# Local attention: dividing the softmax weights on ScalarE ahead of their transposes, instead of turning the divisors and dividing the outputs

## The chip, the cores and the metric

One core of a Trainium2 chip runs the whole kernel in one launch. The metric is the device time of that launch in microseconds (us), as the median of three runs. The engines are named as the profile names them: PE (TensorE, with PEld for its weight loads), DVE (VectorE), ACT (ScalarE), POOL (GpSimd) and SP (the queue that issues DMAs). All data is float32.

## The reference, cut to what matters

The model applies four blocks to x of shape (8, 512, 256), each with its own residual: an attention over all positions (a), a block of two layers of local attention and gated feedforward, a second attention (b), and the local block again. The change touches the local attention only. There, for each of 8 heads of width 64, with windows of 128 positions:

```python
q = l2norm(q) * qs;  k = l2norm(k) * ksc          # then rotary positions
bq = q.reshape(b, h, w, WINDOW, d) * QK_SCALE     # WINDOW = 128, w = 4
bk, bv = look_around(bk), look_around(bv)         # own window and the one before
sim = jnp.einsum('bhwid,bhwjd->bhwij', bq, bk)
sim = jnp.where(mask, -finfo.max, sim)
attn = jax.nn.softmax(sim, axis=-1)
out = jnp.einsum('bhwij,bhwjd->bhwid', attn, bv)
x = x + out.reshape(b, n, INNER) @ wo
```

A query of the first window sees one block of 128 keys, every other query two. The softmax's division can be done on the weights `attn` before the product with v, or on `out` after it.

## The kernel before, in words

The eight batches are worked in two groups of four. A group goes through stages: attention a, local attention and feedforward (twice), attention b, local attention and feedforward (twice). Local attention (`attention_f`) therefore runs eight times: the profile calls them f0x, f0y, f1x and f1y, each name holding two layers.

A stage has 16 tiles of 128 rows (four batches with four windows), and one step for each, with one more step to drain. A step (`a_step`) works on several tiles at once: the attention of tile `step`, the turning of queries and keys of tile `step + 1`, the products of queries, keys and values of tile `step + 2`, and the output projection of tile `step - 1`. `begin`, `rows` and `statistics` prepare the batches that follow. The eight heads of a tile are two units ("even" and "odd" unit), each a `quad` of four heads.

Each unit goes through these functions: `scores` (PE, L586) into PSUM; `maxima` (DVE, L608: adds the mask `near`, takes the maxima; then L618, a product of 128x4 numbers that gives `nm`); `exponentials` (ACT, at L229: four activations, with the sums of the rows as accumulators in `sums`); `turn` (PE, L652: the weights transposed into `ppt`); `keep_turned` (DVE, L663: copied to `pt`); `values` (PE, L677: the outputs, already transposed, into `o`).

For a tile as a whole, `divisors` takes the reciprocals of the sums (DVE, L690) and spreads them over a 128x512 tile `rb` (POOL, L692); `turn_divisors` transposes it (PE, L701, four transposes), `keep_divisors` copies it to `rt` (ACT, L707), and `normalize` multiplies the outputs with it (DVE, L713) to `oT`. `project` (PE, L721) and `add` (DVE, L728) end the tile.

Beside this stand `queries_and_keys` (PE, L489, tile `pqk`), `rotate` (DVE, L517 and L520, then two adds on POOL, L526), `squared` (ACT, L532), `norms` (DVE, L539, then POOL), `value` (PE at L489, tile `pv`, and an ACT copy, L548), `normalize_keys` (DVE, L553), `turn_tile` (PE, L562, tile `pqt`), `keep_tile` (ACT, L571 and L572: `qT` and `kT`) and `started` (two groups of transposes on PE, `pht`, each with an ACT copy, L482, to `hT`).

The order in which the functions stand in `a_step` is the order of each engine's queue: `order_keeper` ties each instruction of an engine to the one before it. Instructions of the next stage (`ahead`) come in at the steps that call it and at the end.

Scores, turned weights, `pqk` and `pqt` share three PSUM buffers (`ps_s`, tag "s"), the smaller products share one (`ps_mm`, tag "mm"), the outputs have one (`ps_o`).

Of the kernel before, what the change touches and what calls it, by code (L numbers as in the profile page):

```python
# [11 lines left out]
F32 = mybir.dt.float32  # L12
AF = mybir.ActivationFunctionType
# [4 lines left out]
P = 128  # L18
# [3 lines left out]
H, HD = 8, 64  # L22
# [22 lines left out]
def kernel(  # L45
# [27 lines left out]
    nc = tc.nc  # L73
# [16 lines left out]
    pool = ctx.enter_context(tc.tile_pool(name="work", bufs=2))  # L90
    ps_s = ctx.enter_context(tc.tile_pool(name="ps_s", bufs=3, space=PSUM))
    ps_mm = ctx.enter_context(tc.tile_pool(name="ps_mm", bufs=1, space=PSUM))
# [91 lines left out]
    ident = const.tile([P, P], F32, name="ident")  # L184
# [282 lines left out]
    def attention_f(batches, l, g, ys, first_layer):  # L467
# [4 lines left out]
        tiles = [(b, t) for b in batches for t in range(NT)]  # L472
        hTs, kTs, vs = {}, {}, {}
        qTs, rns, raws = {}, {}, {}
        ps, pts, sums, os, rts, ots = {}, {}, {}, {}, {}, {}

        def started(b):
            n = f"f{g}_{b}"
# [203 lines left out]
                            stop=(k == nb - 1),  # L682
                        )

        def divisors(at):

            b, w = tiles[at]
            n = f"f{g}_{b}_{w}"
            s = sums.pop(at)
            nc.vector.reciprocal(s, s)  # L690
            rb = pool.tile([P, H, HD], F32, tag="two", name=f"rb_{n}", bufs=5)
            nc.gpsimd.tensor_copy(rb, s.unsqueeze(2).to_broadcast([P, H, HD]))  # L692
            rts[at] = rb

        def turn_divisors(at):
            b, w = tiles[at]
            n = f"f{g}_{b}_{w}"
            rows = rts.pop(at).rearrange("p h d -> p (h d)")
            prt = ps_mm.tile([P, 4, P], F32, tag="mm", name=f"prt_{n}")
            for k in range(4):  # L700
                nc.tensor.transpose(prt[:, k, :], rows[:, k * P : (k + 1) * P], ident)  # L701
            rts[at] = prt

        def keep_divisors(at):
            b, w = tiles[at]
            rt = pool.tile([P, 4, P], F32, tag="two", name=f"rt_f{g}_{b}_{w}", bufs=5)
            nc.scalar.copy(rt, rts[at])  # L707
            rts[at] = rt

        def normalize(at):  # L710
            b, w = tiles[at]
            oT = pool.tile([P, 4, P], F32, tag="two", name=f"oT_f{g}_{b}_{w}", bufs=5)
            nc.vector.tensor_mul(oT, os.pop(at), rts.pop(at))  # L713
            ots[at] = oT

        def project(at):
# [13 lines left out]
        nt, nu = len(tiles), 2 * len(tiles)  # L730

        def on(f, at, count=nt):
            if 0 <= at < count:
                f(at)
# [17 lines left out]
        def a_step(step):  # L752

            even, odd = 2 * step, 2 * step + 1
            on(scores, even, nu)
            on(maxima, even, nu)
            on(queries_and_keys, step + 2)
            on(normalize_keys, step + 1)
            on(exponentials, even, nu)
            on(rotate, step + 2)  # L760
            on(values, even - 1, nu)
            on(turn_divisors, step - 1)
            on(keep_divisors, step - 1)
            on(squared, step + 2)
            on(scores, odd, nu)
            on(maxima, odd, nu)
            on(normalize, step - 1)
            on(turn, even, nu)
            on(keep_turned, even, nu)
            on(value, step + 2)  # L770
            on(norms, step + 2)
            on(turn_tile, step + 1)
            on(exponentials, odd, nu)
            on(keep_tile, step + 1)
            on(project, step - 1)
            on(values, even, nu)
            on(add, step - 1)
            on(divisors, step)
            on(turn, odd, nu)
            on(keep_turned, odd, nu)  # L780
            on(statistics, step + 5)
            on(rows, step + 4)
            on(begin, step + 3)

        def head():
            for step in range(-5, 0):
                a_step(step)
                yield

        def run(ahead):  # L790
            tables_of(EXP_TABLES)
            kept_order = order_keeper()
            for step in range(nt + 1):
                with kept_order():
                    a_step(step)
                    if step == 5 or nt - 6 < step < nt - 1:
                        ahead()
            for _ in range(6):
                ahead()
# [144 lines left out]
    def feedforward_block(batches, g, finish):  # L944

        ys = {}

        def attention(l):
            if l == 0:
                for b in batches:  # L950
                    ys[b] = resid.tile([P, NT, D], F32, tag=f"y{b % GROUP}", name=f"y_{g}_{b}")
            return attention_f(batches, l, f"{g}{l}", ys, l == 0)

        for l in range(DEPTH):
            yield lambda l=l: attention(l)
            yield lambda l=l: feedforward(batches, l, f"{g}{l}", ys, l == DEPTH - 1, finish)
# [500 lines left out]
```

## Time and profile before

| | |
|---|---|
| median of three runs | 4659.25 us (4655.93 to 4671.47) |
| profiled execution, its time and its span | 4656.03 us, 4654.2 us |
| granted TensorE clock over the span | 0.967 |
| PE busy | 4328.7 us, 93% |
| DVE busy | 3179.8 us, 68% |
| ACT busy | 2242.0 us, 48% |
| POOL busy | 1274.8 us, 27% |
| one batch of local attention, four steps (442.69 to 501.54) | 58.85 us |
| PE, DVE, ACT, POOL busy in it | 58.17, 47.07, 31.80, 26.40 us |

Busy times are sums of the instructions' durations on one engine. In the views of the trace a row has the start, the duration, the engine, the line, the operation and the tiles written and read; what stands in brackets is the idle time of that engine before the row, and the work whose end released it. Several instructions of one kind that follow each other are one row with a count. A view of stretches gives for each the busy time and the number of instructions of PE, PEld, DVE, ACT and POOL, then the granted clock.

### The profile page before, as it was taken

Reading aid. Unit: us, or ns where it says so; the run is one execution under the profiler, and the core shown is the slowest. Engines: PE = TensorE matmul, PEld = TensorE weight load, DVE = VectorE, ACT = ScalarE, POOL = GpSimd, SP = SyncE. Lnnn points to the kernel's source line nnn. Section 1 sums busy time; section 2 is a strip of 40 time slices with the busy share of each in tenths; the row PEclk is TensorE's granted clock in tenths of the full one; section 3 lists DMA queues with packets and bytes.
Section 4 is the critical chain, followed back from the end, with each engine's and each line's share of the span. In section 5 each row is a group of like instructions: output and inputs, shape, how many; then the busy total and the mean of one; then the engine's idle time right before and its main releaser. Section 6 shows DMA issues by size and latency. Waiting matters only on the chain.

```text
span 4654.2 us, 68773 instructions
## 1 busy us (share of the span) xinstructions
PE 4328.7 (93%) x26240; PEld 2644.2 (57%) x26240; DVE 3179.8 (68%) x7432; ACT 2242.0 (48%) x5228; POOL 1274.8 (27%) x1164
## 2 busy tenths in 40 slices
PE   9999999997778899999999999999977778999999
PEld 5666656654444466566566666566544444665665
DVE  5667737738988777377456686477389887773773
ACT  3345415516778655155133454254178775541551
POOL 0014314312222243134100242243122222431431
PEclk9999999998889799999999999999999887999999
DMA  2000000000000000000100000000000000000000
GB/s 78 1 21 3 23 22 4 21 6 19 1 1 1 18 4 4 5 22 12 50 29 1 19 3 23 21 3 23 3 20 1 1 1 19 3 5 17 8 3 23
DMA packets 51370, 63.51 MB, mean 14 GB/s; under 512 B 6369, under 2 KB 45793, under 8 KB 51041
## 3 DMA queue, kind: packets, MB, share of 16 engines
q1 hardware_dynamic: 51040, 59.11, 3.9%
q8 instruction: 208, 3.41, 0.3%
q14 instruction: 122, 0.99, 0.1%
HBM read 46.54 MB, written 4.19 MB: 11 GB/s over the span
## 4 chain that ended last, share of the span: by engine, by line
PE 74%; DVE 18%; ACT 5%; POOL 1%; issue 1%; DMA 0%; SPq 0%; POOLq 0%; ACTq 0%; DVEq 0%
DVE num_b L1137 4%; PE pu_g1x L854 3%; PE pu_g0x L854 3%; PE pu_g0y L854 3%; PE pu_g1y L854 3%; DVE r_b L1121 3%; PE s_a L381 3%; DVE pt_b L1172 3%; PE o_a L415 3%; PE ppt_a L398 3%; PE pqk_f0x L489 2%; PE pqk_f1y L489 2%; PE pqk_f0y L489 2%; PE pqk_f1x L489 2%; DVE t_b L1117 2%; PE pu_b L1000 2%
## 5 line engine op out<-in xcount | busy, mean ns | idle before, releaser
L1167 PE MATMUL ppt_b<-ident,num_b 128*128 128x128 f32 x1280 | 245.8, 314 | 195.2 <-DVE pt_b L1172 153.2
L1167 PEld LDWEIGHTS ppt_b<-ident,num_b 128*128 128x128 f32 x1280 | 152.3, 155 | 377.3 <-ACT num_b L229 124.5
L1129 POOL TENSOR_TENSOR num_b<-num_b,causal 128x256 f32<-128x256 f32 (+2 forms) x176 | 172.0, 977 | 699.6 <-ACT num_b L1127 530.7
L229 ACT ACTIVATE p_a<-s_a,nm_a 128x512 f32<-128x512 f32 x256 | 173.6, 683 | 303.0 <-DVE nm_a L385 303.0
L229 ACT ACTIVATE num_b<-num_b,most_b 128x512 f32<-128x512 f32 (+3 forms) x512 | 280.7, 553 | 42.6 <-DVE most_b L1147 40.4
L1137 DVE CUSTOM_DVE_ANT_0 num_b<-num_b,r_b 128x512 f32<-128x512 f32 (+3 forms) x512 | 257.2, 548 | 4.6 <-POOL num_b L1129 4.6
L1098 PE MATMUL den_b<-st_b,st_b 18*128 18x384 f32 (+3 forms) x1024 | 245.1, 531 | 7.6 <-DVE t_b L1117 5.1
L1172 DVE COPY pt_b<-ppt_b 128x512 f32<-128x512 f32 (+1 forms) x352 | 223.1, 634 | 25.1 <-PE ppt_b L1167 23.8
L229 ACT ACTIVATE r_b<-den_b 128x1024 f32<-128x1024 f32 (+1 forms) x176 | 166.2, 945 | 149.2 <-PE den_b L1098 93.8
L1098 PE MATMUL dot_b<-st_b,st_b 16*128 16x384 f32 (+3 forms) x1024 | 218.9, 533 | 1.6 <-ACT num_b L1127 1.1
L229 ACT ACTIVATE p_f1y<-p_f1y,nm_f1y,rn_f1y 128x256 f32<-128x256 f32 (+1 forms) x256 | 143.7, 564 | 136.1 <-DVE nm_f1y L618 124.5
L229 ACT ACTIVATE p_f0y<-p_f0y,nm_f0y,rn_f0y 128x256 f32<-128x256 f32 (+1 forms) x256 | 143.7, 563 | 133.9 <-DVE nm_f0y L618 122.2
L229 ACT ACTIVATE p_f1x<-p_f1x,nm_f1x,rn_f1x 128x256 f32<-128x256 f32 (+1 forms) x256 | 143.7, 564 | 129.8 <-DVE nm_f1x L618 112.6
L229 ACT ACTIVATE p_f0x<-p_f0x,nm_f0x,rn_f0x 128x256 f32<-128x256 f32 (+1 forms) x256 | 143.7, 563 | 129.1 <-DVE nm_f0x L618 117.5
L1117 DVE TENSOR_TENSOR t_b<-den_b,r_b 128x1024 f32<-128x1024 f32 (+1 forms) x176 | 196.6, 1117 | 11.5 <-ACT r_b L229 10.5
L1121 DVE SCALAR_TENSOR_TENSOR r_b<-t_b,r_b 128x1024 f32<-128x1024 f32 (+1 forms) x176 | 197.8, 1124 | 0.1
L385 DVE TENSOR_REDUCE nm_a<-s_a 128x2 f32<-128x1024 f32 x128 | 156.1, 1220 | 61.0 <-PE s_a L381 59.8
L229 ACT ACTIVATE r_b<-r_b 128x1024 f32<-128x1024 f32 (+1 forms) x176 | 172.4, 980 | 5.5
L398 PEld LDWEIGHTS ppt_a<-ident,p_a 128*128 128x128 f32 x1024 | 109.9, 141 | 98.1 <-ACT p_a L229 39.7
L1127 ACT ACTIVATE num_b<-dot_b 128x1024 f32<-128x1024 f32 (+1 forms) x176 | 164.6, 935 | 0.0
L400 DVE COPY pt_a<-ppt_a 128x1024 f32<-128x1024 f32 x128 | 155.4, 1214 | 2.6 <-PE ppt_a L398 2.5
L854 PE MATMUL pu_g0x<-hT_g0x,wg_0x 128*128 128x512 f32 (+1 forms) x352 | 156.6, 592 | 0.0
(361 smaller groups left out, 11025.1 us busy)
## 6 DMA issues: line engine op xcount, KB each, us to landing
x<-in_x SPq DMA_DIRECT2D x8, 512.0 KB
out<-x SPq DMA_DIRECT2D x8, 512.0 KB
wf_0x<-in_f_wqkv SPq DMA_DIRECT2D x2, 1536.0 KB
wf_0y<-in_f_wqkv SPq DMA_DIRECT2D x2, 1536.0 KB
wf_1x<-in_f_wqkv SPq DMA_DIRECT2D x2, 1536.0 KB
wf_1y<-in_f_wqkv SPq DMA_DIRECT2D x2, 1536.0 KB
wg_0x<-in_f_w SPq DMA_DIRECT2D x2, 1386.0 KB
wg_0y<-in_f_w SPq DMA_DIRECT2D x2, 1386.0 KB
```

Of the source, the lines that this page charges most:

```text
L229: i = nc.scalar.activation(out, in_, func, **more).ins
L398: nc.tensor.transpose(ppt[:, odd, k, :], p[:, odd, k * P : (k + 1) * P], ident)
L489: nc.tensor.matmul(dst.rearrange("p h d -> p (h d)"), lhsT=hTs[b][:, k, t * P : (t + 1) * P], rhs=wqkv[:, k, c * INNER : (c + 1) * INNER], ...
L854: nc.tensor.matmul(pu[: cols.stop - cols.start, c], lhsT=w1[:, k, cols], rhs=hT[:, k, :], start=(k == 0), stop=(k == 1),)
L1098: return nc.tensor.matmul(s[:, a, m * width : (m + 1) * width], lhsT=left[at, j, past:width], rhs=right[at, j, :width], start=True, stop=True,
L1117: nc.vector.tensor_mul(t[:, :, :cols], den[:, :, :cols], r[:, :, :cols])
L1121: nc.vector.scalar_tensor_tensor(r[:, :, :cols], t[:, :, :cols], 2.0, r[:, :, :cols], ALU.subtract, ALU.mult)
L1127: nc.scalar.activation(num[:, :, :cols], dot[:, :, :cols], AF.Square, scale=-0.5)
L1129: nc.gpsimd.tensor_add(own, own, causal.unsqueeze(1).unsqueeze(1).to_broadcast([P, 2, len(js), P]))
L1137: nc.vector.tensor_tensor_reduce(out=s4[:, a, m, :], in0=s4[:, a, m, :], in1=r4[:, a, m, :], scale=-1.0, scalar=LOWEST, op0=ALU.mult, op1= ...
L1167: nc.tensor.transpose(ppt[:, k, :], p[:, a, k * P : (k + 1) * P], ident)
L1172: nc.vector.tensor_copy(pt[:, a, :nblocks, :], ppt[:, :nblocks, :])
```

## The change

The divisors are no longer spread, turned and multiplied into the outputs. A new function `divided` takes the reciprocals of one unit's four sums on VectorE, and ScalarE multiplies the unit's weights with them in place, one activation (identity with a scale for each row) for each head, before the weights are turned. `keep_values` then only copies the outputs out of PSUM. The order of the step is written anew: the odd unit's weights are turned at the start of the next step, and the values' product and the other parts stand at other places.

```diff
-        def divisors(at):
-            ...
-        def turn_divisors(at):
-            ...
-        def keep_divisors(at):
-            ...
-        def normalize(at):
+        def divided(unit):
+
+            at, quad = divmod(unit, 2)
+            p, s = ps[unit], sums[at]
+            some = slice(4 * quad, 4 * quad + 4)
+            nc.vector.reciprocal(s[:, some], s[:, some])
+            for odd in range(2):
+                for j in range(2):
+                    h = 4 * quad + 2 * j + odd
+                    nc.scalar.activation(p[:, odd, j], p[:, odd, j], AF.Identity, scale=s[:, h : h + 1])
+
+        def keep_values(at):
             b, w = tiles[at]
             oT = pool.tile([P, 4, P], F32, tag="two", name=f"oT_f{g}_{b}_{w}", bufs=5)
-            nc.vector.tensor_mul(oT, os.pop(at), rts.pop(at))
+            nc.vector.tensor_copy(oT, os.pop(at))
             ots[at] = oT
...
             on(scores, even, nu)
             on(maxima, even, nu)
+            on(turn, even - 1, nu)
+            on(normalize_keys, step + 1)
+            on(keep_turned, even - 1, nu)
             on(queries_and_keys, step + 2)
-            on(normalize_keys, step + 1)
             on(exponentials, even, nu)
+            on(divided, even, nu)
             on(rotate, step + 2)
             on(values, even - 1, nu)
-            on(turn_divisors, step - 1)
-            on(keep_divisors, step - 1)
             on(squared, step + 2)
             on(scores, odd, nu)
             on(maxima, odd, nu)
-            on(normalize, step - 1)
+            on(value, step + 2)
+            on(exponentials, odd, nu)
+            on(keep_values, step - 1)
             on(turn, even, nu)
             on(keep_turned, even, nu)
-            on(value, step + 2)
             on(norms, step + 2)
             on(turn_tile, step + 1)
-            on(exponentials, odd, nu)
             on(keep_tile, step + 1)
             on(project, step - 1)
+            on(divided, odd, nu)
             on(values, even, nu)
             on(add, step - 1)
-            on(divisors, step)
-            on(turn, odd, nu)
-            on(keep_turned, odd, nu)
             on(statistics, step + 5)
             on(rows, step + 4)
             on(begin, step + 3)
```

## The prediction

> **What bounds the kernel now.** The page's busy line comes first, then stretches of one stage. A stage is one layer of local attention (8 run, f0x to f1y with two layers each); its steps take one tile of 128 rows each, and one batch is four steps, w = 0 to 3. Below, w0 to w3 are the steps whose scores belong to that tile; w0 has one block of 128 keys, the others two. The third stretch is one batch, the other two are its steps w1 and w3 as the trace cuts them.
>
> ```profile
> PE 4328.7 (93%) x26240; PEld 2644.2 (57%) x26240; DVE 3179.8 (68%) x7432; ACT 2242.0 (48%) x5228; POOL 1274.8 (27%) x1164
> ...
> 456.46:470.14 13.68, 13.68 (x78) 8.40 (x80) 12.71 (x33) 7.54 (x21) 5.81 (x4) 1.00 0.00 0
> 486.71:501.54 14.83, 14.83 (x98) 9.68 (x100) 11.47 (x29) 7.93 (x22) 6.27 (x6) 1.00 0.00 1
> 442.69:501.54 58.85, 58.17 (x370) 37.52 (x372) 47.07 (x125) 31.80 (x87) 26.40 (x24) 1.00 0.00 1
> ```
>
> TensorE is busy in the whole of such a step (14.83 of 14.83 us), VectorE 11.5, ScalarE 7.9, GpSimd 6.3. "Busy" alone would not prove a bound, so I read the order of time. In a w3 step:
>
> ```profile
> 488.65 1.14 PE L586 MATMUL s_f0x<-kT_f0x,qT_f0x 64*128 64x256 f32 x8
> 489.71 3.70 PE L489 MATMUL pqk_f0x<-wf_0x,hT_f0x 128*128 128x512 f32 x8
> 493.45 1.22 DVE L517 TENSOR_TENSOR ro_f0x<-pqk_f0x,tab 128x1024 f32<-128x1024 f32 x1 [1.30 <-PE pqk_f0x L489]
> 494.37 0.66 PE L701 MATMUL prt_f0x<-ident,rb_f0x 128*128 128x128 f32 x4
> 495.95 2.50 POOL L526 TENSOR_TENSOR ro_f0x<-ro_f0x,rs_f0x 128x512 f32<-128x512 f32 x2 [5.51 <-DVE rs_f0x L520]
> 497.64 0.84 DVE L618 SCALAR_TENSOR_TENSOR nm_f0x<-nm_f0x,rn_f0x 128x4 f32<-128x4 f32 x1
> 498.40 0.68 DVE L713 TENSOR_TENSOR oT_f0x<-o_f0x,rt_f0x 128x512 f32<-128x512 f32 x1
> 499.54 1.96 PE L721 MATMUL pp_f0x<-wf_0x,oT_f0x 128*128 128x256 f32 x8
> ```
>
> Each PE row begins where the one before it ends: S (scores) 1.06, QK 3.63, V (values) 1.03, the turned divisors 0.58, S 1.07, T (turned weights) 0.93, the value product PV 1.72, the turned tile PQT 0.87, PP (projection) 1.89, then V and T again; 14.83 in all. So TensorE sets this step. But see a second chain: rotation starts 3.74 after QK (493.45), GpSimd's two adds run 495.95 to 498.45, and the tiny `nm` product of 128x4 takes 0.84 us instead of 0.16 because it ends only with them; L713 waits behind it. In the w1 step this chain is already the tighter one:
>
> ```profile
> 462.33 1.23 DVE L517 TENSOR_TENSOR ro_f0x<-pqk_f0x,tab 128x1024 f32<-128x1024 f32 x1 [0.25 <-PE pqk_f0x L489]
> 466.16 1.20 DVE L618 SCALAR_TENSOR_TENSOR nm_f0x<-nm_f0x,rn_f0x 128x4 f32<-128x4 f32 x1
> 467.28 0.68 DVE L713 TENSOR_TENSOR oT_f0x<-o_f0x,rt_f0x 128x512 f32<-128x512 f32 x1
> 468.11 1.97 PE L721 MATMUL pp_f0x<-wf_0x,oT_f0x 128*128 128x256 f32 x8
> ```
>
> `nm` asks 0.08 us after GpSimd's first add has ended (466.08) and pays the whole second one, 1.20 us. From the rotation's start to the projection's are 5.78 us, of which no part is slack: PP starts 0.15 after its operand. From QK's start that is 3.74 + 5.78 = **9.52 us**; in the w3 step TensorE itself needs 9.83 (489.71 to 499.54). The cover is 0.31.
>
> **What the Trainium skill says.** "SBUF — State Buffer", section "SBUF: two separate sides": the port pair of VectorE and GpSimd is an exclusive lock for a whole instruction, and a VectorE op with two SBUF inputs waits behind a GpSimd op that reads SBUF. The trace agrees (0.84 and 1.20 against 0.16). "ScalarE: Activation LUTs", section "What ACT_TABLE_LOAD costs": an ACTIVATE takes 186 ns + 0.833 ns per element, each pointer operand adds 93 ns, and neighbours overlap by 93 ns. The trace agrees where it can: an exp of 256 elements with two pointers took 590 ns (186 + 213 + 186 = 585). The same page, "Table sets", says that identity is in every set, so no table load is added; no run yet shows it. "PSUM — Partial Sum Buffer", "PSUM bank collisions raise a hardware error", says that two engines must not read a bank together; here Square (L532) indeed starts only when the rotation has ended (495.96 after 495.87).
>
> **The parts.** (1) Removed from each of 128 steps: four transposes on PE (0.58), one PSUM copy on ACT (0.58), one GpSimd copy (0.61). (2) VectorE: one reciprocal (0.19) becomes two; the product L713 (0.68) becomes a PSUM copy of the same size (L663 at 128x512: 0.68). (3) ScalarE gains eight identities. By the price above 186 + 213 + 93 = 492 ns each, 0.40 apart; I take 0.40 (estimate from the page). Bounds: 0.31 if the pointer is free, 0.585 if it costs what an exp with its accumulator does. ScalarE then has 7.9 - 0.6 + 3.2 = 10.5 of 14.5 us: not a bound by sum. (4) Waits: the reciprocal of the even unit stands on VectorE ahead of the rotation and waits for the exps; the identities of the odd unit stand on ScalarE ahead of the next batch's hT copies, and the turn of the odd unit moves to the next step's start, which covers them there. No DMA and no SP instruction moves; GpSimd's queue only loses its copy.
>
> **The new step, walked from S (even) at 0.** Maxima start 1.25 (489.90 - 488.65), exps 3.02, ends of the accumulators 5.48 (494.12 before). The reciprocal follows at 5.51, rotation may start at 5.61. In w2 and w3: S 1.06, T of the last odd unit 1.02, so QK starts at 2.06 and the rotation is due at 2.06 + 3.74 = 5.80: the new wait is hidden by QK with 0.2 to spare. From QK to PP, TensorE now needs 9.83 - 0.58 = 9.25, but the rotation chain still needs 9.52. So PP starts at 11.58, then 1.89 + 1.03 give **14.50** against 14.83: -0.33, not -0.58. Does anything else bind? Odd exps start 0.12 after `nm`, at 5.80 + 5.03 + 0.12 = 10.95; qT at 13.29, kT done at 14.33; the next S needs it at 14.50: fits by 0.17. Identities run 14.21 to 15.9; the turn in the next step starts its four pairs at 15.56, 15.8, 16.1, 16.3: fits at 0.40 each.
>
> w1: the turn ahead of QK belongs to w0 and is short (0.59), so QK starts at 1.65 and the rotation would be due at 5.39; the reciprocal holds it to 5.61. PP at 5.61 + 5.78 = 11.39, where TensorE would have been ready at about 10.6; V ends at 14.31. Then come the two transposes of the next batch with a ScalarE copy between, through one PSUM buffer:
>
> ```profile
> 471.96 0.60 PE L283 MATMUL pht_f0x<-ident,y_0x 128*128 128x128 f32 x4
> 472.59 0.58 ACT L482 COPY hT_f0x<-pht_f0x 128x512 f32<-128x512 f32 x1 [1.41 <-PE pht_f0x L283]
> 473.23 0.65 PE L283 MATMUL pht_f0x<-ident,y_0x 128*128 128x128 f32 x4 [0.68 <-ACT hT_f0x L482]
> ```
>
> Before, ScalarE was free and this cost 473.82 - 471.96 = 1.86. Now the copy stands behind the odd identities: exps 10.76, qT 13.10, kT 13.56, identities 14.02 to 15.62; copy 15.62 to 16.20, second turn 16.26, next S 16.84. Before: 473.82 - 457.53 = 16.29. So **+0.55**.
>
> w0: loses the divisors (0.59) and its own odd turn (0.59), gains w3's (1.02); -0.16, and 0.2 more in a first layer, where PQT waited for Square, which the later rotation of w1 behind the rows' normalization (1.66 on VectorE) gives back. Its `nm` is ready earlier and gets in between GpSimd's two adds, as before (0.50), so no bubble.
>
> A batch: -0.16 + 0.55 - 0.33 - 0.33 = **-0.27**. A stage has three such, then w0 (-0.2) and w1 without the hT copies (-0.1). Its tail loses: without QK the steps are a pure chain, and the even identities (1.6) now stand between the even and the odd exps. Step 14 takes 12.8 by the same walk (odd maxima 6.95, odd exps 8.73, oT 9.2, PP 9.3, V 11.2, a turn for the next stage 12.2) against 544.08 - 532.68 = 11.4; the last step and the drain 18.05 against 17.6. Together +1.9. Bounds: 0 if the gated stage's products fill the gaps, +3 if none does. Stage: -0.8 - 0.3 + 1.9 = +0.8; eight stages **+6.4 us**. Everything else is untouched.
>
> The profiled execution took 4656.03 us (span 4654.2); the sum gives 4662.4. It lies 3.2 below the median of the runs (4659.25), so for a median I say **4666**. 0.3% is 14 us, about what a measurement of this kernel can tell from no change.
>
> **Rivals.** *The saving shows (faster).* It needs the rotation chain to loosen: if `nm` asks 0.1 us earlier it ends with GpSimd's first add, 1.25 earlier. Then w2 and w3 reach 14.25, w1 16.0 to 16.2: a batch is near -1.4 to -1.6, a stage 3 x -1.5 - 1.0 + 1.9 = -3.6, all -29 us: 4630; with the tail's cover too, -44: 4615. The bare floor, 128 x 0.58 = 74 us, isn't reached. For it: the margin is 0.08. Against: w1 shows the miss every time, and the order there is the new one. Chance 0.32.
>
> *The identities are dear (slower).* The place is ScalarE's queue at a step's end. Above 0.53 each, the turn at 1.06 of the next step waits: at 0.585 by 0.2 us a step, the hT copies by 4 x 0.185 = 0.74 a batch: a batch +1.3, a stage 3.9 + 0.6 + 2.5 = 7, all +56: 4715. Between 0.45 and 0.5 with the dear tail, +20 to +30: 4680 to 4690. For it: no identity with a pointer is in the trace, and each new wait is walked with little to spare (0.2, 0.17). Against: the page's price. Chance 0.40 of being over +14.
>
> *It doesn't do what it says:* identity missing from the set would add loads of 1.28 us each (the page's 20 loads took 25.7) hundreds of times; inside the slower case, under 0.02.
>
> **How the numbers follow.** The walk's own case, within 14 us, has 0.28: its centre is +6, but a term of 0.1 us a step is 13 us. The likeliest by its own bounds (identity 0.31 to 0.49, tail 0 to 3) spans 4641 to 4688. The range reaches into both rivals, 4620 to 4698, and leaves about 0.2 outside.
>
> **What would show it.** Right: PE busy falls by some 74 us but the span doesn't; `nm` of odd units at 1.2 us, PE idle ahead of L721 by 0.2 in w2 and w3 and by 0.8 in w1; the second transpose of hT waiting 1.3 us instead of 0.7; w2 and w3 at 14.50, batches near 58.4 (58.85 before). Wrong: w3 at 14.25, or `nm` at 0.5 and less (the first rival); identities 0.5 apart and PE waiting for them at the turn (the second).

## The result and the profile after

The changed kernel takes **4689.15 us** (median of 4 runs, 4683.71 to 4691.68) against 4657.85 for the kernel before beside it (4 runs, 4655.93 to 4671.47): a ratio of 1.0059, 95% interval 1.0038 to 1.0080. It is slower by 0.6%, twice what the measurement can tell from no change. Run once more on another occasion it took 4685.90, a ratio of 1.0041 (1.0029 to 1.0054). The forecast was 4666 in a range of 4620 to 4698, with 0.40 for slower, 0.32 for faster.

The profiled execution took 4683.71 us, its span is 4681.9 (before: 4656.03 and 4654.2), so **27.7 us** of span are to be explained; every split of it below is of these two executions. The granted TensorE clock is 0.960 (before 0.967). The page's busy line:

```profile
PE 4267.5 (91%) x25728; PEld 2608.4 (56%) x25728; DVE 3208.6 (69%) x7560; ACT 2575.3 (55%) x6124; POOL 1209.6 (26%) x1036
```

TensorE has 512 instructions less (4 x 128) and is busy for 61.2 us less, while the span grows. One batch of local attention, and its steps w1 and w2, in stretches that begin with a step's first scores (columns: length, busy time of PE, PEld, DVE, ACT, POOL with the number of instructions, clock, DMA share, GB/s):

```profile
441.74:499.67 57.93, 55.59 (x356) 35.79 (x354) 47.71 (x129) 42.20 (x116) 24.61 (x19) 1.00 0.00 1
454.98:471.70 16.72, 14.63 (x91) 9.23 (x89) 12.39 (x33) 12.23 (x33) 8.07 (x5) 1.00 0.00 0
471.70:486.09 14.39, 14.26 (x94) 9.28 (x93) 11.86 (x29) 9.99 (x26) 3.27 (x6) 1.00 0.01 2
```

The batch is 0.92 us *shorter* than before (58.85), although the kernel is slower. TensorE no longer fills its steps: 2.1 us of w1 are idle. The w2 step in order of time:

```profile
473.69 3.60 PE L489 MATMUL pqk_f0x<-wf_0x,hT_f0x 128*128 128x512 f32 x8
477.12 0.18 DVE L690 RECIPROCAL sums_f0x<-sums_f0x 128x4 f32<-128x4 f32 x1 [0.84 <-ACT p_f0x L229]
477.33 1.23 DVE L517 TENSOR_TENSOR ro_f0x<-pqk_f0x,tab 128x1024 f32<-128x1024 f32 x1
477.33 1.71 ACT L694 ACTIVATE p_f0x<-p_f0x,sums_f0x 128x256 f32<-128x256 f32 x4 [0.25 <-DVE sums_f0x L690]
479.89 2.51 POOL L526 TENSOR_TENSOR ro_f0x<-ro_f0x,rs_f0x 128x512 f32<-128x512 f32 x2 [8.07 <-DVE rs_f0x L520]
481.15 1.27 DVE L618 SCALAR_TENSOR_TENSOR nm_f0x<-nm_f0x,rn_f0x 128x4 f32<-128x4 f32 x1
482.34 0.68 DVE L699 COPY oT_f0x<-o_f0x 128x512 f32<-128x512 f32 x1
483.17 1.97 PE L707 MATMUL pp_f0x<-wf_0x,oT_f0x 128*128 128x256 f32 x8
```

From QK (L489) to the rotation 3.64 us, from the rotation to the projection 5.84: the chain of the prediction, with the `nm` product of 128x4 now at 1.27 us. The turned tile starts at 482.00 and takes 0.87 where nothing follows late (498.67 to 499.54 before), so TensorE is free at 482.87 and waits 0.30 for the projection's operand. (Rows of TensorE overlap a little; by their own ends the gap is 0.13.) Four identities take 1.71 us. In w1 the same chain is later still, and the hT copy waits behind the odd unit's identities:

```profile
464.28 1.27 DVE L618 SCALAR_TENSOR_TENSOR nm_f0x<-nm_f0x,rn_f0x 128x4 f32<-128x4 f32 x1
466.30 1.97 PE L707 MATMUL pp_f0x<-wf_0x,oT_f0x 128*128 128x256 f32 x8 [0.85 <-DVE oT_f0x L699]
468.88 1.71 ACT L694 ACTIVATE p_f0x<-p_f0x,sums_f0x 128x256 f32<-128x256 f32 x4
470.49 0.57 ACT L482 COPY hT_f0x<-pht_f0x 128x512 f32<-128x512 f32 x1
471.11 0.66 PE L283 MATMUL pht_f0x<-ident,y_0x 128*128 128x128 f32 x4 [1.24 <-ACT hT_f0x L482]
```

So the full steps behave as walked, and gain. The loss lies in the stages' ends and in the clock. Step 13 is the last w1 of a stage, step 14 the w2 after it. Steps from scores to scores in one second-layer stage (f0y), before and after: w1 16.29 and 16.72, w2 and w3 14.83 and 14.39, w0 12.68 and 12.44; but step 13 takes 16.14 and 16.76, step 14 11.40 and **12.69**, and from the last step's scores to the feedforward's first output (the row y, DVE L900, after L885) 42.32 and **44.24**. From the last feedforward's row of this kind to its own, that stage is 259.61 and 260.85 long, and it is the only one of the four second-layer stages that is so short after: the others take 262.4 to 262.9. What they have more is seen by setting the same place of two stages side by side. First stretches of 3.41 us, then TensorE's rows, of f0x (near 900) and f0y (near 2200):

```profile
896.57:899.98 3.41, 0.93 (x17) 0.85 (x16) 2.54 (x8) 2.45 (x8) 0.00 (x0) 1.00 0.00 0
899.98:903.39 3.41, 3.41 (x20) 2.32 (x15) 1.12 (x6) 1.71 (x4) 0.00 (x0) 0.50 0.00 0
2197.20:2200.61 3.41, 1.67 (x14) 1.08 (x12) 3.11 (x12) 1.26 (x4) 1.49 (x1) 1.00 0.00 0
2200.61:2204.02 3.41, 2.67 (x29) 2.13 (x30) 1.33 (x5) 3.17 (x10) 0.00 (x0) 1.00 0.00 0
```

```profile
899.12 1.19 PE L677 MATMUL o_f0x<-pt_f0x,v_f0x 128*64 128x128 f32 x16 [2.48 <-DVE pt_f0x L663]
900.24 2.08 PE L586 MATMUL s_f0x<-kT_f0x,qT_f0x 64*128 64x256 f32 x8
902.25 1.63 PE L652 MATMUL ppt_f0x<-ident,p_f0x 128*128 128x128 f32 x8
...
2201.34 1.09 PE L677 MATMUL o_f0y<-pt_f0y,v_f0y 128*64 128x128 f32 x16 [2.48 <-DVE pt_f0y L663]
2202.37 1.14 PE L586 MATMUL s_f0y<-kT_f0y,qT_f0y 64*128 64x256 f32 x8
2203.43 1.10 PE L652 MATMUL ppt_f0y<-ident,p_f0y 128*128 128x128 f32 x8
```

The wait is the same 2.48 us in both. In f0x it falls into one stretch, TensorE is busy there for 0.93 of 3.41 us, and the next stretch is granted half the clock (0.50): scores take 2.08 instead of 1.14, and the projection comes 1.03 later. In f0y the wait is split over two stretches and nothing happens. The clock's records of one execution all lie on one grid of 3.413 us, placed differently in each execution. Between the first and the last oT copy of its eight stages the changed kernel has 11 such half-clock stretches, about 1.0 us each; the kernel before has one.

The 27.7 us, from the trace: the stages without half-clock stretches **+8.4** (from the first oT copy to the last 209.74 in an undisturbed stage, against the eight lengths of before less their 1.6 of half clock: +2.8 in sum; and 0.69 up to the first oT copy, measured in the second layers and taken eight times); half clock in the stages **+9.4** (11.0 after, 1.6 before); the two stretches with attention b **+10.9**, whose code is untouched (more on them below); attention a -1.0; the feedforwards 0.0.

### The profile page after: what moved, and what is told of

It is laid out like the page before. It is cut to its first block, busy times and chain, and to the rows that moved or that the text cites. A ratio compares the mean times of both kernels' runs of the same rounds, so it can differ in the third digit from the quotient of the medians.

```text
span 4681.9 us, 68609 instructions
## 1 busy us (share of the span) xinstructions
PE 4267.5 (91%) x25728; PEld 2608.4 (56%) x25728; DVE 3208.6 (69%) x7560; ACT 2575.3 (55%) x6124; POOL 1209.6 (26%) x1036
## 5 line engine op out<-in xcount | busy, mean ns | idle before, releaser
L839 PE MATMUL pu_g1x<-hT_g1x,wg_1x 128*128 128x512 f32 (+1 forms) x352 | 157.2, 593 | 0.0
```

What stands on the lines that cost most here:

```text
L839: nc.tensor.matmul(pu[: cols.stop - cols.start, c], lhsT=w1[:, k, cols], rhs=hT[:, k, :], start=(k == 0), stop=(k == 1),)
```

## The experiments

All ratios are against the kernel before, run beside each kernel on the same chip (its medians there: 4657.85 to 4664.46). The step columns are from scores to scores in one second-layer stage; the last column counts the half-clock stretches between the first and the last oT copy of the eight stages in the profiled execution. Ahead of the first copy, from a stage's first scores on, each profile has 3 to 7 more (7 in e_split, 3 before and 3 after).

| kernel | median us | ratio (95%) | w1 | w2, w3 | w0 | step 14 | half clock |
|---|---|---|---|---|---|---|---|
| before | 4657.85 | 1 | 16.29 | 14.83 | 12.68 | 11.40 | 1 |
| changed | 4689.15 | 1.0059 (1.0038-1.0080) | 16.72 | 14.39 | 12.44 | 12.69 | 11 |
| e_split | 4633.39 | 0.9926 (0.9912-0.9939) | 15.63 | 14.03 | 12.45 | 12.70 | 3 |
| e_before_split | 4665.86 | 1.0006 (0.9998-1.0014) | 16.16 | 14.83 | 12.68 | 11.40 | 2 |
| e_nodiv | 4634.42 | 0.9935 (0.9923-0.9948) | 16.34 | 14.58 | 12.10 | 11.26 | 6 |
| e_noid | 4648.27 | 0.9967 (0.9955-0.9979) | 15.87 | 14.39 | 12.32 | 12.70 | 12 |
| e_hT | 4672.71 | 1.0020 (1.0012-1.0027) | 16.28 | 14.39 | 12.43 | 12.70 | 9 |
| e_tail | 4666.57 | 1.0006 (0.9998-1.0014) | 16.71 | 14.39 | 12.44 | 12.44 | 2 |
| e_turn2 | 4690.44 | 1.0057 (1.0044-1.0070) | 16.72 | 14.39 | 12.44 | 12.84 | 14 |
| e_fill | 4675.36 | 1.0024 (1.0015-1.0032) | 16.72 | 14.39 | 12.44 | 12.70 | 2 |
| after_again | 4685.90 | 1.0041 (1.0029-1.0054) | 16.73 | 14.39 | 12.44 | 12.70 | 9 |
| e_all | 4616.92 | 0.9893 (0.9879-0.9906) | 15.18 | 14.03 | 12.44 | 12.44 | 0 |
| e_best | 4585.46 | 0.9829 (0.9816-0.9843) | 13.74 | 14.46, 14.03 | 12.44 | 12.44 | 1 |

### The chain over `nm`: e_split, e_before_split, e_nodiv

```diff
-                nc.gpsimd.tensor_add(ro[:, c], ro[:, c], rs[:, c])
+                for some in (slice(0, 4), slice(4, 8)):
+                    nc.gpsimd.tensor_add(ro[:, c, some], ro[:, c, some], rs[:, c, some])
```

> The changed kernel with each of GpSimd's two rotation adds of 128x512 cut in two of 128x256, so that the odd unit's nm product can get in after some 0.65 us in place of 1.27. Theory (rotation to projection by way of nm binds w1, and w2 and w3 by little): nm falls from 1.27 to 0.4-0.7, TensorE's wait ahead of the projection in w1 from 0.85 to 0.2, w1 by some 0.6, w2 and w3 by 0.1 each: 24 to 32 batches x 0.8 = -20 to -25 us: 4663-4670. Rival (TensorE is the bound, the chain has slack or the next wait is as long): nm falls and the span does not, 4685-4690; or slower by GpSimd's two more instructions per step if the rotated block is then late.

Measured: 4633.39, 55.8 us under the changed kernel, more than twice the expected gain. The rows of w2 in e_split:

```profile
478.06 2.79 POOL L527 TENSOR_TENSOR ro_f0x<-ro_f0x,rs_f0x 128x256 f32<-128x256 f32 x4 [8.07 <-DVE rs_f0x L520]
...
479.33 0.17 DVE L619 SCALAR_TENSOR_TENSOR nm_f0x<-nm_f0x,rn_f0x 128x4 f32<-128x4 f32 x1
479.42 0.68 DVE L700 COPY oT_f0x<-o_f0x 128x512 f32<-128x512 f32 x1
...
481.05 1.89 PE L708 MATMUL pp_f0x<-wf_0x,oT_f0x 128*128 128x256 f32 x8
```

GpSimd's four short adds take 2.79 instead of 2.51, but `nm` gets in between them and takes 0.17 instead of 1.27, and oT is ready 0.95 before the projection starts (479.42 + 0.68 against 481.05). TensorE is then busy in the whole of w2 (14.03 of 14.03). The Trainium skill, "SBUF — State Buffer", section "SBUF: two separate sides", has the port pair locked for a whole instruction; that the price of the lock falls with the length of GpSimd's instruction is what these rows show. My expectation took TensorE's own work at 14.25 (0.1 to 0.2 a step to gain); back to back it is 14.03. A batch falls by 1.80 (57.94 to 56.14), 24 of them by 43 us, step 13 by 1.07 in each of eight stages, and eight half-clock stretches fewer make about 8. Against that, the first w1 of four stages takes 17.0: a half-clock stretch lies there that the changed kernel doesn't have.

The same cut in the kernel before:

> The kernel before (divisors turned as before) with GpSimd's rotation adds cut in two, as it helped the changed kernel by 55 us. Theory (in the kernel before TensorE sets w2 and w3 by 0.31 ahead of the chain, only w1 waits for nm): w3 stays at 14.83 to 14.6, w1 falls from 16.3 by 0.6 to 0.9, 24 batches x 0.8 = -15 to -20 and so 4640-4650; then the change's own gain with short adds (4633 against this) is real, but small. Rival (the cut is worth the same in both, 55 us, and the change costs 25 us in either): 4605-4610.

Measured: 4665.86, no change. w1 falls by 0.13 (16.29 to 16.16) and w2, w3 by nothing. The expectation of 0.6 to 0.9 in w1 was wrong: TensorE stood idle ahead of the projection for only 0.13 there, and then its own work sets the step. The rival (55 us in either kernel) was further off. So these two edits gain only together: the cut alone +0.06%, the change alone +0.4 to 0.6%, both -0.7%.

The third kernel is the one before with the divisors taken out:

```diff
-            nc.vector.tensor_mul(oT, os.pop(at), rts.pop(at))
+            nc.vector.tensor_copy(oT, os.pop(at))
...
-            on(turn_divisors, step - 1)
-            on(keep_divisors, step - 1)
...
-            on(divisors, step)
```

> The kernel before without the divisors, their turning and their copies; what the values gave is only copied to SBUF (left out: the division by the softmax sums). Nothing is put in their place: no identities, the order else as before. Theory (as predicted: the chain rotation, GpSimd's adds, nm, oT, projection holds w2 and w3, with 0.31 of cover): w3 falls from 14.83 by 0.3, to 14.5, not by 0.58; w1 stays at 16.3, as nm is as late as before: a batch -0.9, all about -25 to -35: 4630. Rival (TensorE's work is the bound): each step -0.58, w3 14.25, all -74: 4585-4590.

Measured: 4634.42, as the theory had it (4630), far from the rival's 4585-4590. TensorE has 0.58 less to do in each step and gets 0.25 of it in w2 and w3 (14.58), none in w1 (16.34). Two rows of w2:

```profile
482.14 1.27 DVE L618 SCALAR_TENSOR_TENSOR nm_f0x<-nm_f0x,rn_f0x 128x4 f32<-128x4 f32 x1
```

```profile
484.15 1.97 PE L721 MATMUL pp_f0x<-wf_0x,oT_f0x 128*128 128x256 f32 x8 [0.18 <-DVE oT_f0x L713]
```

With no identity anywhere, `nm` takes 1.27 and TensorE waits for oT. Removing TensorE's work is by itself worth 29 us of 74; in w1 to w3 the reason is the one given in the prediction.

### What the identities cost in the new order: e_noid

```diff
-            on(divided, even, nu)
...
-            on(divided, odd, nu)
```

> The changed kernel without the reciprocals and the identities (left out: the division by the softmax sums), the order else as changed. Theory (in the full steps the identities lie beside other work save the hT copy's 0.5 in w1 and the rotation behind the reciprocal, 0.2; at the stage's start and in its tail they stand in the chain): batches fall by 0.5 to 0.8, the start by 0.7, the tail by 2 to 3, no half-clock stretches at the stages' ends: a stage -5 to -6, all -40 to -50: 4640-4650. Rival (the new order and not the identities makes the tail dear): the tail stays within 0.5 of 62.6, all -15 to -20: 4670.

Measured: 4648.27, 41 us under the changed kernel. w2 and w3 don't move (14.39): there the identities are free. The batch falls by 0.97 (56.97 against 57.94), nearly all of it in w1. With the shortest value that each step has among the eight stages, which leaves the half clock out, a stage is 5.0 shorter than the undisturbed one of the changed kernel (expected 5 to 6), eight of them 40 us; the tail's share from step 13 on is 2.0. But step 14 stays at 12.70: this part of the tail is the new order's and not the identities'. And 12 half-clock stretches are left where none were expected, since the wait in step 14 is left. The drain, too, stays long: where no half clock lies in it, 43.71 from the last scores to the feedforward's first output, 0.53 less than with the identities and 1.39 more than before. No identity waits behind the table load any more, but the projection waits 1.45 for oT instead of 0.73:

```profile
1841.86 1.99 PE L707 MATMUL pp_f0y<-wf_0y,oT_f0y 128*128 128x256 f32 x8 [1.45 <-DVE oT_f0y L699]
1843.76 1.28 ACT L223 ACT_TABLE_LOAD   x1
```

e_nodiv and e_noid hold the same number of instructions on every engine (PE 25728, DVE 7304, ACT 5100, GpSimd 1036) and differ in their order alone. So the medians split the change in three: the divisors' work goes, -29 us (4663.73 to 4634.42); the new order, +14 (to 4648.27); the identities with their reciprocals, +38 to +41 (to 4685.90 or 4689.15). In the order's share the full steps gain (0.64 a batch), while step 14 and the drain lose 1.44 and 2.81 against e_nodiv (11.26 and 40.90), and there are 12 half-clock stretches against 6.

### The hT copy and the tails' order: e_hT, e_tail

```diff
-                nc.scalar.copy(hT[:, k, k : k + T], transposed(ps_mm, halves_of(ys[b]), k, f"pht_{n}_{k}"))
+                nc.vector.tensor_copy(hT[:, k, k : k + T], transposed(ps_mm, halves_of(ys[b]), k, f"pht_{n}_{k}"))
```

> The changed kernel with the copy of the turned normalized rows (hT, two per batch of four steps) on VectorE in place of ScalarE, where it stands behind the odd unit's identities. Theory (the hT copy behind the identities costs w1 +0.55): the second turn waits 0.7 us in place of 1.24 behind the first, w1 falls by 0.5 to 1.2, 12 batches turn hT twice in every layer: 24 batches x 0.6 to 1.0 = -15 to -25 us: 4665-4675. Rival (VectorE is as late at that place, its queue then holds keep_values or the maxima up): within 5 us of the changed kernel. Rival (tails and clock only): no change, 4685-4690.

Measured: 4672.71, -16 us; w1 16.72 to 16.28. The second turn waits 0.78 instead of 1.24:

```profile
473.56 0.66 PE L283 MATMUL pht_f0x<-ident,y_0x 128*128 128x128 f32 x4 [0.78 <-DVE hT_f0x L482]
```

```diff
+            if step >= nt - 2:
+                on(scores, even, nu)
...
+                on(exponentials, even, nu)
+                on(scores, odd, nu)
+                on(maxima, odd, nu)
+                on(values, even - 1, nu)
+                on(divided, even, nu)
+                on(turn_tile, step + 1)
...
+                on(exponentials, odd, nu)
...
+                return
```

> The changed kernel with another order in the last two steps and the drain of each stage alone (step 14 on): the odd unit's scores and maxima ahead of the values of the unit before, the turned tile ahead of the odd exps. Theory (the tails carry the loss: dearer chain there, and TensorE idle at 534.31 for 1.59 us, after which the granted clock halves for 3.4 us): the half-clock stretches at the stages' ends become fewer (some 11 in the changed kernel), step 14 falls from 12.6-14.8 to some 11.5, each stage's tail by 2 to 3 us, all 15 to 25 us less than the changed kernel: about 4665-4675. Rival (the loss is the full steps' waits, the new rotation wait and hT): nothing moves by more than 5 us: 4685-4690. Rival (the spread of attention b's clock decides): the tails may shorten, the whole follows attention b's spans.

Measured: 4666.57, -23 us. TensorE's wait in step 14 is shorter, since the odd scores come ahead of it:

```profile
897.79 1.13 PE L586 MATMUL s_f0x<-kT_f0x,qT_f0x 64*128 64x256 f32 x8
900.35 1.09 PE L677 MATMUL o_f0x<-pt_f0x,v_f0x 128*64 128x128 f32 x16 [1.42 <-DVE pt_f0x L663]
```

The undisturbed stage falls by only 0.9 (260.85 to 259.96), 7 us in eight stages; 2 half-clock stretches in place of 11 make about 9 more. Step 14 reached 12.44, not the expected 11.5. The rest of the 23 is not taken apart. So the gain came more from the clock than from the chain.

### The clock by itself: e_turn2, e_fill, after_again

```diff
-            for odd in range(2):
+            for again in range(2 if quad == 0 and at >= nt - 2 else 1):
+                for odd in range(2):
...
```

> The changed kernel with more work for TensorE and none taken away: in steps 14 and 15 of each stage the even unit's weights are turned twice into the same place (8 transposes, 0.93 us more, 16 times in all: +15 us of TensorE). They fall into a stretch in which TensorE waits 2.48 us (1.87 in step 15) for the turned weights' copy, which VectorE starts only 1.8 us after the turn, behind the odd unit's maxima and the keys' normalization. Theory (the clock: in the changed kernel a stretch of 3.41 us on a fixed grid in which TensorE is busy for less than 45% is followed by one at half clock, each of which makes the step about 1.0 us longer; 11 of them in the stages): filled to over 50% these windows go, step 14 is 12.75 everywhere in place of 12.75 to 13.93, and the whole is some 11 us shorter in spite of the added work: about 4676-4680. Rival (the tail is only a chain of waits): no change where the copy still comes last, or up to 15 us longer: 4689-4704.

Measured: 4690.44, no change, and 14 half-clock stretches. It tells nothing of the theory, because I had filled the wrong place:

```profile
530.50 1.09 PE L653 MATMUL ppt_f0x<-ident,p_f0x 128*128 128x128 f32 x8
534.07 1.62 PE L678 MATMUL o_f0x<-pt_f0x,v_f0x 128*64 128x128 f32 x16 [2.48 <-DVE pt_f0x L664]
535.62 2.08 PE L586 MATMUL s_f0x<-kT_f0x,qT_f0x 64*128 64x256 f32 x8
537.63 2.07 PE L653 MATMUL ppt_f0x<-ident,p_f0x 128*128 128x128 f32 x16
```

The doubled turn (x16) stands behind the wait; the turn ahead of it is that of the *odd* unit of the step before. The condition for the right place:

```diff
+            for again in range(2 if quad == 1 and at == nt - 3 else 1):
```

> The double turn again, now in the right place: the stretch in which TensorE waits 2.48 us in step 14 comes after the turn of the odd unit of step 13, so this one alone is turned twice (8 transposes, 0.93 us, 8 times in all: +7.4 us of TensorE). Its copy starts 1.2 us after the turn's end, so 0.93 fit without moving it. Theory (the clock): stretches of the 3.41 us grid that were busy for some 27% come to over 50%, and none of them is followed by half clock; step 14 is 12.75 in all eight stages in place of up to 14.58 (7.6 us in the changed kernel's profile); the half-clock stretches of step 15 (busy for 45%) stay. All -5 to -9 against the changed kernel run beside it. Rival (the tail is only a chain of waits): 0 to +7.

Measured: 4675.36, **10.5 us less than the changed kernel run beside it (4685.90), by adding 64 transposes.** The runs overlap (4669.64 to 4684.61 in 14, 4677.85 to 4689.87 in 5); their means lie 8.4 apart, give or take 7. What happened is plainer in the profile. The stretch that holds the wait, and TensorE's rows in it:

```profile
894.73:898.15 3.42, 2.61 (x24) 2.02 (x20) 3.12 (x12) 1.27 (x4) 1.56 (x1) 1.00 0.00 0
898.15:901.56 3.41, 2.62 (x29) 2.07 (x30) 1.33 (x5) 3.17 (x10) 0.00 (x0) 1.00 0.00 0
```

```profile
895.37 1.97 PE L653 MATMUL ppt_f0x<-ident,p_f0x 128*128 128x128 f32 x16
898.94 1.09 PE L678 MATMUL o_f0x<-pt_f0x,v_f0x 128*64 128x128 f32 x16 [1.60 <-DVE pt_f0x L664]
```

The wait is 1.60 instead of 2.48, the values still come 4.63 after the scores (894.31), as before the filling; the time between oT copies in step 14 is 12.75 in all eight stages (12.75 to 14.58 in the changed kernel). Two half-clock stretches are left, both in step 15.

> The changed kernel once more, for the spread of its clock. Theory: full steps to the number (16.86, 14.38, 12.87, 13.82), the half-clock stretches at the stages' ends elsewhere and in another number (8 to 14), attention b between 578 and 589 us a time as in the other kernels, whichever they are. 4686-4692, 1.004 to 1.007 of the kernel before. Rival (attention b is made slower by the change): both attention b stretches over 583 again.

Measured: 4685.90. The full steps repeat to 0.02 us (the expectation counts them from oT copy to oT copy). Half clock in the stages costs 9.4 us again (9 stretches), at other places: step 14 is 12.75 in one stage and 14.38 in the next. The two stretches up to the first oT copy behind attention b take 588.7 and 588.5.

### Everything together: e_all, e_best

> The changed kernel with the three edits together: the tails' order, hT on VectorE, GpSimd's adds cut in two. Theory (three separate losses): the sum of the three, some -50 us less a part for what they share: 4635-4650, which beats both kernels. Rival (one loss seen from three sides): no better than the best of the three alone. Rival (the clock takes back what the order gives): the span falls by less than half the sum, with the granted clock lower.

Measured: 4616.92, better than expected, as e_split alone had been. The three gains (56, 16 and 23) add up to 95, together they give 72: e_split and e_tail had each got rid of most half-clock stretches already, which accounts for some 8 of the 23; the rest is not taken apart. TensorE is idle in a batch only for the 0.78 between the two hT turns.

```diff
+        def started_too(b):
+            nc.scalar.copy(hTs[b][:, 1, 1 : 1 + T], transposed(ps_mm, halves_of(ys[b]), 1, f"pht_f{g}_{b}_1"))
...
             on(scores, even, nu)
+            on(begin_too, step + 2)
```

> The kernel with the three edits (adds cut in two, hT on VectorE, tails in another order), and the second of the two hT turns moved behind the next step's first scores, its copy on ScalarE. In the three-edit kernel TensorE idles only there in a batch of four steps (0.78 of 55.67 us). Theory: the wait goes, a batch 54.9, 24 x 0.78 = -18 us: about 4598, the best so far. Rival (ScalarE is then late with the copy, still behind the odd identities, and the next query and key product waits): 4610-4620, no gain.

Measured: **4585.46**, 0.9829 of the kernel before (0.9816 to 0.9843), 104 us under the changed kernel. The profile shows the second turn without a wait:

```profile
709.05 1.13 PE L589 MATMUL s_f0x<-kT_f0x,qT_f0x 64*128 64x256 f32 x8
710.12 0.66 PE L283 MATMUL pht_f0x<-ident,y_0x 128*128 128x128 f32 x4
710.61 1.04 PE L655 MATMUL ppt_f0x<-ident,p_f0x 128*128 128x128 f32 x8
```

A batch takes 13.74 + 14.46 + 14.03 + 12.44 = 54.67 us, 1.0 less than in e_all (55.67; 0.78 expected), and 4.0 less than before (58.63). 24 batches make 24 of the 31 us under e_all; the two stretches with attention b, which no edit touches, happen to be 10.8 shorter in its profile (583.6 and 580.3 against 588.9 and 585.8), so the margin over the expected 4598 is in part their spread.

## Why the prediction was right, and where it wasn't

**The rotation chain (w2, w3): right.** Forecast 14.50, `nm` at 1.2, TensorE idle by 0.2 ahead of the projection; measured 14.39, 1.27 and 0.30. The 0.11 are in TensorE's products: QK's start is 0.07 earlier and the rotation follows it by 3.64 instead of 3.74, while the way from there to the projection is 0.06 longer. e_nodiv and e_split show the cause from both sides: with less work alone a step gains 0.25 of 0.58 and TensorE waits for oT, with the shorter lock it waits for nothing.

**w1 and the hT copy: right.** Forecast 16.84 (+0.55), PP waiting 0.8, the second turn 1.3; measured 16.72, 0.85 and 1.24. e_hT takes 0.44 of it away.

**The price of an identity: right.** The estimate of 0.40 apart from the Trainium skill ("ScalarE: Activation LUTs", "What ACT_TABLE_LOAD costs") gives 0.49 + 3 x 0.40 = 1.69 for four; the trace has 1.71. The rival "the identities are dear" has the right side and the wrong price: it needed 0.45 and more each. What they cost comes from where they stand, about 40 us by e_noid.

**The batch: too small a gain.** Forecast -0.27, measured -0.92 in first layers (58.85 to 57.93) and -0.69 in second ones. The terms: w0 -0.46 (first layers) or -0.24 for -0.16, w1 +0.43 for +0.55, w2 and w3 -0.44 each for -0.33.

**The tail: too small a loss, and its reason wrong.** Forecast +1.9 a stage: step 14 +1.4 and last step with drain +0.45. Measured in f0y: step 13 +0.62 (I had -0.1 for it), step 14 +1.29, last step and drain +1.92. The walk put the loss down to the even identities between the even and the odd exps. e_noid takes them out, and step 14 stays at 12.70: there the right number was luck. TensorE's long wait in it, 2.48 for the turned weights' copy, is in both, and in the changed kernel ScalarE even stands idle for 1.20 between the identities and the odd exps. In the drain 1.39 of the 1.92 stay in e_noid and belong to the new order. The other 0.53 are the identities', which now stand behind the load of the feedforward's activation table; before, nothing waited there for ScalarE:

```profile
2219.80 1.28 ACT L223 ACT_TABLE_LOAD   x1
2221.09 1.71 ACT L694 ACTIVATE p_f0y<-p_f0y,sums_f0y 128x256 f32<-128x256 f32 x4
```

No load is added, as forecast (20 in both profiles). Step 13 is the identities' own: without them it takes 15.24, with them 16.76. TensorE waits there 0.55 for Square ahead of the turned tile and 1.09 for oT ahead of the projection.

**The sum of the walk: near, because the two errors offset each other.** +0.8 a stage and +6.4 in all were forecast; the undisturbed stage f0y has +1.24, and the eight +8.4.

**What the prediction left out: the clock.** It counted waits of TensorE at their length. In the tails they also cost clock: +9.4 us in the changed kernel's profile. That this is a cause and not a companion is shown by e_fill. The Trainium skill, "TensorE: Matmul & The Clock Gate", Part 1, describes a free-running window of about 3.4 us whose idleness halves the clock, and warns of idle gaps beyond 3.4 us; here gaps of 1.9 to 2.5 us are enough, if they fall well into one window. I had read the granted clock only as a mean. In e_fill step 14 has none in any stage; the stretches of step 15 were left alone. TensorE's busy time fell by 61.2 instead of the 74 named as a sign; its products last longer at half clock, but how much of the 13 this makes was not split up.

**Attention b: spread from run to run, as far as can be told.** The two stretches from a feedforward's end over attention b to the first oT copy take 580.2 and 578.2 in the profile of before and 583.7 and 587.0 after. In the 13 profiles they lie between 578.2 and 588.9; two kernels with the order of before have 584.5 and 581.8, 586.7 and 582.3, one with the new order has 588.5 and 578.7. The profile of before lies at the low end. Their length goes with the number of half-clock stretches in them, 41 to 53 (correlation 0.89 over the 26; 88 in the two of before, 97 in the two after), so most of the 10.9 is probably clock again; no run varied it. A small share of the change (3 us on average, within the spread) can't be excluded.

**The number: inside the range by its width.** The walk speaks of 8.4 of the 27.7 us. The other 19 are half clock and attention b, for which the prediction had no term. That 4689 lies within 4620 to 4698 is owed to an upper end drawn out for dear identities; the case that the prediction called its own, within 14 us of no change, did not come (+31).

**The rival "the saving shows"** had its condition spelt out: `nm` freed from GpSimd's second add gives 4630, with the tail's cover 4615. e_split made the condition true: 4633, and with the tails and hT 4617. The mechanism held, and the totals came close, though by other sums: a batch fell by 2.5 (58.63 to 56.14) where 1.4 to 1.6 were written down, and the tail and the clock took the rest back; the margin of 0.08 us did not open by itself.

## What to carry to other kernels

Before work is taken from the busiest engine, measure the second chain that runs level with it: here it had 0.31 us of cover in a step, so of 0.58 saved only 0.25 to 0.44 showed, until the instruction that locked the port was cut in two; the cut by itself was worth nothing, and both together 0.7%. A new order has to be walked where the pipeline drains, too, and apart from the new instructions: here the order alone made step 14 and the drain 1.4 and 2.8 us longer (e_nodiv to e_noid). And where TensorE begins to wait, look at the granted clock in short stretches: a tail that idles is paid twice.

## What the hardware showed that I had not expected

In the stages of all 13 profiles, between the first and the last oT copy, a grid stretch of 3.413 us in which TensorE was busy for less than 43% was followed by one at half clock in 33 of 33 cases; between 43% and 47% in 23 of 39; between 47% and 55% in 2 of 40; above 55% in 14 of some 6200. These fourteen hold less work than their share says. Five ran at half clock themselves (84 to 86% busy). In the other nine (57 to 64%) a turn waits for the exps pair by pair, so that its eight transposes fill 2.2 us in place of 0.93, as in the kernel before ahead of its one half-clock stretch:

```profile
4155.00 2.19 PE L652 MATMUL ppt_f1y<-ident,p_f1y 128*128 128x128 f32 x8 [0.24 <-ACT p_f1y L229]
```

A step at a fixed place of the program is so up to 1.8 us longer or not, by where the grid happens to lie (step 14, 12.75 to 14.58).

How long a group of TensorE's products takes, from its start to the next one's, goes with what stands ahead of it: QK takes 3.63 us behind scores and 3.53 behind turned weights, the value product 1.72 behind turned weights and 1.82 behind scores; the projection 1.89 where its operand comes while the turned tile runs (499.08 in w3 of before) and 1.82 where it is there ahead of that tile (480.10 in e_split). In the w2 step of e_split the sum is 14.03 instead of the 14.25 that the rows of before gave: the two turns of weights take 1.80 together in place of 1.95, the projection 0.07 less. No run varied this by itself.
